# Five row buffers over the keys, the second set's scatters spread over the tiles, and the first set's results fetched two tiles sooner

## The chip, the cores and the metric

The kernel runs on one core of a Trainium2 chip. The core has five engines with an instruction queue each: TensorE (PE) multiplies, VectorE (DVE) and ScalarE (ACT) do elementwise work, GpSimd (POOL) does small elementwise work and issues the DMAs whose row addresses are data (indirect DMAs), and SyncE (SP) issues the plain DMAs. Each queue is worked off in its order; engines wait for each other by semaphores. The metric is the device time of one execution in microseconds: a median of 1357.8 over three runs of the kernel before, 1356.98 to 1358.16.

## The reference

One transformer block on 2 x 1024 rows of 256 numbers, all float32: an attention with 16 query heads and one key/value head, and a mixture of 8 experts of which each row uses 2. Both stand behind a layer norm with a shift and a scale computed from a condition `c`, and both are added to `x` through a gate.

```python
mod = (silu(c) @ wmod).reshape(2, 6, 1, -1)        # sa, ca, ga, sb, cb, gb
h = layernorm(x) * (1 + ca) + sa
x = x + ga * attention(h)      # q, k normalised; 16 heads; out @ Wout; layernorm
h = layernorm(x) * (1 + cb) + sb
# experts
logits = h @ router_w.T
topk_vals, topk_idx = top_k(logits, 2)
topk_w = softmax(topk_vals)
x_sorted = h[order // 2]                           # rows sorted by expert
y1 = ragged_dot(x_sorted, w1, counts);  gate, up = split(y1, 2)
y2 = ragged_dot(silu(gate) * up, w2, counts)
y = (y2[inv] * topk_w).sum over the two choices
x = x + gb * y
```

## The kernel before

**Attention.** The 2048 rows are 16 row tiles of 128, and four query blocks of four tiles. For each block, `attention` (L469) runs over 16 heads and 8 key tiles: a score matmul (L478), its exponential on ScalarE (L482), a product with the values (L493). The keys of all rows lie transposed in one buffer, `kT` (8 KB in each partition); it stands first in the pool `big`, ahead of `vs` and the queries `qT`. `project` (L541) multiplies a block's heads by `Wout` (L547); `Settle` then normalises the result, adds it to `xs` (`residual`, L587), takes the second layer norm (`norms`, `logits`), the router's logits, and the two chosen experts with their weights (`weights`, L630).

**Sorting.** Each row goes to two experts. Where it stands in the list sorted by expert is counted in `count` and `bases`, and `scatter` (L741) writes a row tile of `rows` (256 numbers, the weight, the row that the result belongs to, and the batch) to those places in DRAM with an indirect DMA from POOL. There are two sets, so that the experts can begin before the last block is through: set 0 holds row tiles 0 to 11 and gives 31 sorted tiles of 128 rows, set 1 holds row tiles 12 to 15 (the last block) and gives 15. Set 0 is scattered during the last block's attention. For set 1 all of `residual`, `norms`, `logits`, `weights`, `count`, `bases` and its scatters take place in the expert stage, between the tiles. Its scatters come in two lots of four, one lot for each of a row's two choices; `choose_second` (L759) on POOL overwrites the weight and the destination in `rows` between the lots, and so waits until the first lot has been read.

**The expert stage.** It works through 46 sorted tiles in a loop over `m` (L1015). In step `m`, tile `m` is loaded seven steps ahead (`PRE`) and transposed (`turn`: xp on PE, its copy xT on ACT); tile `m-1` is multiplied by its expert's `w1` (`up`: su on PE, sg on ACT, sact on DVE); tile `m-3` is transposed back (`turn_back`: ap on PE, sactT on ACT); tile `m-4` (`LAG`) is multiplied by `w2` (`down`: sy on PE), scaled by weight and gate on DVE into `ysb` (L963, `self.evicted`), and written to its rows of `results` in DRAM by an indirect DMA from POOL (L966). `ysb` has four buffers and the PSUM tile `sy` two.

**Buffers.** The expert stage's pools take over the memory of the attention's. Three row tiles have buffers of their own outside both (`EARLY`, pool `mx`), and are loaded before the attention is over. All others, and the fetched results, share the 18 buffers of the pool `mr` (`row_buffer`, L887), which lie over `qT` and over the `proj` tile that `project` fills and `residual` reads.

**The results.** `fetch` (L987) reads the two results of each row of a row tile from DRAM (256 KB, SP queue), which is possible once all scatters of its set have landed; `combine` (L1001) adds both and `xs` on DVE, and writes the output (SP queue). For set 0 the loop fetches from m = 38 on, four row tiles in three steps (L1046), and combines each two steps later, behind the DVE instruction `evicted` of tile `m-4` (`tc.issue_after`). Set 1's four are fetched and combined after the loop.

The order within an engine's queue is made by a scheduler from the program's order, from dependencies and from these `issue_after` hints.

Of the kernel before, what the change touches and what calls it, by code (L numbers as in the profile page):

```python
# [38 lines left out]
FP = mybir.dt.float32  # L39
# [6 lines left out]
P = 128  # L46
# [9 lines left out]
def tile_adaln_attention_moe(  # L56
# [24 lines left out]
    QT = QB // P  # L81
# [8 lines left out]
    TOP = 2  # L90
    SETS = ((0, (NBLK - 1) * QT), ((NBLK - 1) * QT, NT))

    def tiles_for(n):

        return (TOP * n * P + E * (P - 1)) // P

    NM = [tiles_for(t1 - t0) for t0, t1 in SETS]
# [13 lines left out]
    WEIGHT, TO, BATCH, ROW = D, D + 1, D + 2, D + 4  # L111
# [5 lines left out]
    place_i = keep.tile([P, NT, TOP], I32, name="place_i")  # L117
# [82 lines left out]
    class Scattered:  # L200
# [3 lines left out]
        def __init__(self, name):  # L204
            self.name, self.all = name, []
# [19 lines left out]
    EARLY = 3  # L225
    mx = ctx.enter_context(tc.tile_pool(name="mx", bufs=1))

    with ExitStack() as attn:
# [440 lines left out]
        def count(blk, filled, work, psum, tag):  # L669

            t0 = blk * QT
            n = QT * TOP
            pairs = chosen[:, t0 : t0 + QT].rearrange("p t k e -> p (t k) e")
            ps = psum.tile([P, 2, n, E], FP, tag=tag, name=f"count_{blk}")
            for i, m in enumerate((before, ones)):
                nc.tensor.matmul(
                    ps[:, i].rearrange("p n e -> p (n e)"),
                    m,
                    pairs.rearrange("p n e -> p (n e)"),
                    start=True,  # L680
                    stop=True,
                )
            own = work.tile([P, n, E], FP, tag="z", name=f"own_{blk}")
            for i in range(n):
                nc.vector.tensor_tensor(own[:, i], ps[:, 0, i], filled, ALU.add)
                nc.vector.tensor_tensor(filled, filled, ps[:, 1, i], ALU.add)
            nc.vector.tensor_tensor(own, own, pairs, ALU.mult)
            nc.vector.tensor_reduce(
                place[:, t0 : t0 + QT].rearrange("p t k -> p (t k)"), own, AX.X, ALU.add
            )  # L690
# [50 lines left out]
        def scatter(to, i, t):  # L741
            ins = nc.gpsimd.indirect_dma_start(
                out=sorted_x[i],
                out_offset=bass.IndirectOffsetOnAxis(ap=to, axis=0),
                in_=rows[:, t, :],
                in_offset=None,
            )
            into_x[i].add(ins)
# [10 lines left out]
        def choose_second(t0, t1):  # L759

            nc.gpsimd.tensor_copy(rows[:, t0:t1, WEIGHT], share[:, t0:t1])
            nc.gpsimd.tensor_copy(rows[:, t0:t1, TO].bitcast(I32), second_to[:, t0:t1])
# [102 lines left out]
        w1_sb, w2s = w1_at  # L865

    with ExitStack() as moe:
        mg = moe.enter_context(tc.tile_pool(name="mg", bufs=3))
        ms = moe.enter_context(tc.tile_pool(name="ms", bufs=2))
        RING = 18  # L870
# [15 lines left out]
        PRE = 7  # L886
        def row_buffer(name):  # L887


            return mr.tile([P, TOP * D], FP, tag="x", name=name)  # L890

        class Sorted:


            def __init__(self, i, m):
                self.i, self.at = i, m
                self.m = m + sum(NM[:i])
                if self.m < EARLY:
                    self.x = mx.tile([P, ROW], FP, name=f"x_{self.m}")
                else:  # L900
                    self.x = row_buffer(f"x_{self.m}")[:, :ROW]
                load = nc.sync.dma_start(out=self.x, in_=sorted_x[i][ts(m, P), :])
                into_x[i].read(load)
# [40 lines left out]
            def down(self):  # L944
                m = self.m
                at = nc.values_load(
                    at_w2[self.i][0:1, self.at : self.at + 1],
                    engines=[mybir.EngineType.PE],
                    min_val=0,
                    max_val=(E - 1) * 2 * D,  # L950
                    skip_runtime_bounds_check_because="the expert's number is clamped",
                )
                y = ps_y.tile([P, D], FP, tag="y", name=f"sy_{m}")
                for c in range(2):
                    nc.tensor.matmul(  # L955
                        y,
                        self.actT[:, c, :],
                        w2_flat[:, c * D :][:, bass.ds(at, D)],
                        start=(c == 0),
                        stop=(c == 1),  # L960
                    )
                ysb = mg.tile([P, D], FP, tag="ysb", name=f"ysb_{m}", bufs=4)
                self.evicted = nc.vector.scalar_tensor_tensor(  # L963
                    ysb, y, self.x[:, WEIGHT : WEIGHT + 1], self.gate, ALU.mult, ALU.mult
                )
                ins = nc.gpsimd.indirect_dma_start(  # L966
                    out=results[self.i],
                    out_offset=bass.IndirectOffsetOnAxis(
                        ap=self.x[:, TO : TO + 1].bitcast(I32), axis=0
                    ),  # L970
                    in_=ysb,
                    in_offset=None,
                )
                into_results[self.i].add(ins)

            def gates(self):
# [10 lines left out]
        def fetch(t):  # L987

            i = 0 if t < SETS[0][1] else 1
            at = t - SETS[i][0]  # L990
            y = row_buffer(f"y_{t}").rearrange("p (k d) -> p k d", k=TOP)
            load = nc.sync.dma_start(
                out=y,
                in_=results[i][TOP * at * P : TOP * (at + 1) * P, :].rearrange(
                    "(p k) d -> p k d", k=TOP
                ),
            )
            into_results[i].read(load)
            return y

        def combine(t, y):  # L1001

            res = my.tile([P, D], FP, tag="res", name=f"res_{t}")
            nc.vector.tensor_tensor(res, y[:, 0, :], y[:, 1, :], ALU.add)
            nc.vector.tensor_tensor(res, res, xs[:, t, :], ALU.add)
            nc.sync.dma_start(out=ot[:, t, :], in_=res)
# [4 lines left out]
        which = [(i, m) for i, n in enumerate(NM) for m in range(n)]  # L1011
        tiles = []
        fetched, have = [], 0
        LAG = 4
        for m in range(len(which) + LAG):  # L1015
            while len(tiles) < min(m + 1 + PRE, len(which)):
                tiles.append(Sorted(*which[len(tiles)]))
            if m < len(tiles):
                tiles[m].turn()
            if 0 <= m - 1 < len(tiles):  # L1020
                tiles[m - 1].up()
            if 0 <= m - 3 < len(tiles):
                tiles[m - 3].gates()
                tiles[m - 3].turn_back()
            if 0 <= m - LAG < len(tiles):
                tiles[m - LAG].down()

            if m < QT:
                settle.residual(m, m + 1)
            elif m == QT:  # L1030
                settle.norms()
            elif QT < m <= 2 * QT:
                settle.logits(m - QT - 1)
            elif m == 2 * QT + 1:
                settle.weights()
            elif m == 2 * QT + 2:
                count(NBLK - 1, filled[1], mg, ps_t, "t")
            elif m == 2 * QT + 3:
                bases(1, mg)
                for k in range(TOP):  # L1040
                    if k:
                        choose_second(*SETS[1])
                    for t in range(*SETS[1]):
                        scatter(place_i[:, t, k : k + 1], 1, t)

            n = (m - (len(which) - 1 - PRE) + 1) * 4 // 3  # L1046
            for t in range(have, min(n, SETS[0][1])):
                fetched.append((m, t, fetch(t)))
                have = t + 1
            while fetched and fetched[0][0] <= m - 2:  # L1050
                with tc.issue_after(tiles[m - LAG].evicted.ins):
                    combine(*fetched.pop(0)[1:])
# [50 lines left out]
```

## Time and profile before

| what | value |
|---|---|
| median of three runs | 1357.8 us (1356.98 to 1358.16) |
| the profiled execution | 1363.5 us |
| its span, first to last instruction | 1361.8 us |
| PE busy | 1326.3 us, 97% |
| DVE / ACT / POOL busy | 685.6 / 489.0 / 229.4 us |
| PE's share of the chain that ended last | 93% |
| granted PE clock, mean | 0.989 |
| result scatters (L966, POOL) | 46, 1021 ns each |
| row loads (L902, SP) | 46 of 130 KB |
| result fetches (L992, SP) | 16 of 256 KB |

The span has four parts that can be told apart in the timeline: a start to about 60 us in which PE waits at times for loads and norms, the four attention blocks, the last block's out-projection until 1215.5 us, and the expert stage until the end. "The chain that ended last" is followed back from the last instruction, at each step to what released it. In the row of 40 slices each digit is the busy share of a slice of 34 us in tenths:

```
PE   7899999999999999999999999999999999989895
POOL 4200212110100000000100000001001233003543
```

### The profile page before, as it was taken

Reading aid. Unit: us, or ns where it says so; the run is one execution under the profiler, and the core shown is the slowest. Engines: PE = TensorE matmul, PEld = TensorE weight load, DVE = VectorE, ACT = ScalarE, POOL = GpSimd, SP = SyncE. Lnnn points to the kernel's source line nnn. Section 1 sums busy time; section 2 is a strip of 40 time slices with the busy share of each in tenths; the row PEclk is TensorE's granted clock in tenths of the full one; section 3 lists DMA queues with packets and bytes.
Section 4 is the critical chain, followed back from the end, with each engine's and each line's share of the span. In section 5 each row is a group of like instructions: output and inputs, shape, how many; then the busy total and the mean of one; then the engine's idle time right before and its main releaser. Section 6 shows DMA issues by size and latency. Waiting matters only on the chain.

```text
span 1361.8 us, 12740 instructions
## 1 busy us (share of the span) xinstructions
PE 1326.3 (97%) x4024; PEld 688.8 (51%) x4024; DVE 685.6 (50%) x1380; ACT 489.0 (36%) x954; POOL 229.4 (17%) x325
## 2 busy tenths in 40 slices
PE   7899999999999999999999999999999999989895
PEld 4444444446544444447444444466444444467674
DVE  6346655544545554533646454545465545347445
ACT  2433344442243333331343333422433333314342
POOL 4200212110100000000100000001001233003543
PEclk9899999999999999999999999999999999999998
DMA  7001000000004310101000210000000122013335
GB/s 243 1 0 31 1 32 0 20 12 32 1 1 156 57 32 0 31 1 32 0 1 31 85 32 1 31 32 0 1 32 0 55 65 91 1 43 118 122 124 191
DMA packets 46322, 59.18 MB, mean 43 GB/s; under 512 B 10672, under 2 KB 32432, under 8 KB 46256
## 3 DMA queue, kind: packets, MB, share of 16 engines
q1 hardware_dynamic: 42512, 48.08, 11.6%
q0 software_dynamic: 3744, 10.29, 2.1%
q8 instruction: 33, 0.54, 0.2%
q14 instruction: 33, 0.27, 0.1%
HBM read 39.69 MB, written 18.66 MB: 43 GB/s over the span
## 4 chain that ended last, share of the span: by engine, by line
PE 93%; DVE 2%; POOL 1%; DMA 1%; issue 1%; ACT 0%; another core or an unknown queue 0%; SPq 0%; POOLq 0%; DVEq 0%; ACTq 0%
PE s L478 32%; PE o L493 32%; PE q L441 8%; PE pr L547 7%; PE su L924 4%; PE sy L955 3%; PE qp L455 2%; PE den L507 1%; PE kv L384 1%; PE xp L909 1%; PE ap L940 1%; PE lg L625 0%; POOL rn_q L178 0%; PE warm_a L768 0%
## 5 line engine op out<-in xcount | busy, mean ns | idle before, releaser
L478 PE MATMUL s<-qT,kT 128*128 128x512 f32 x1024 | 525.3, 595 | 0.1
L493 PE MATMUL o<-p,vs 128*128 128x512 f32 x1024 | 522.7, 593 | 0.0
L482 ACT ACTIVATE p<-s 128x512 f32<-128x512 f32 x512 | 305.6, 597 | 502.4 <-PE s L478 487.1
L498 DVE TENSOR_TENSOR sum<-sum,p 128x512 f32<-128x512 f32 x384 | 264.3, 688 | 180.1 <-ACT p L482 175.6
L493 PEld LDWEIGHTS o<-p,vs 128*128 128x128 f32 x1024 | 193.4, 190 | 233.2 <-issue 232.0
L478 PEld LDWEIGHTS s<-qT,kT 128*128 128x128 f32 x1024 | 187.3, 191 | 206.2 <-issue 204.2
L177 POOL TENSOR_SCALAR rn_q<-rn_q 128x4 f32<-128x4 f32 x64 | 14.0, 219 | 719.9 <-DVE rn_q L344 704.8
L441 PE MATMUL q<-wq_sb,rows 128*128 128x512 f32 x256 | 121.0, 596 | 0.0
L547 PE MATMUL pr<-wout_sb,qT 128*128 128x256 f32 x512 | 112.7, 380 | 0.0
L547 PEld LDWEIGHTS pr<-wout_sb,qT 128*128 128x128 f32 x512 | 96.6, 190 | 18.9 <-issue 4.3
L498 DVE TENSOR_TENSOR sum<-p,p 128x512 f32<-128x512 f32 x64 | 44.2, 690 | 112.7 <-ACT p L482 112.6
L344 DVE TENSOR_REDUCE rn_q<-sq_q 128x4 f32<-128x512 f32 x64 | 43.8, 684 | 83.6 <-ACT sq_q L343 83.6
L178 POOL TENSOR_TENSOR rn_q<-rn_q,minus_half 128x4 f32<-128x4 f32 x64 | 83.3, 1302 | 5.3
L441 PEld LDWEIGHTS q<-wq_sb,rows 128*128 128x128 f32 x256 | 49.0, 192 | 60.4 <-issue 50.4
L347 DVE TENSOR_TENSOR vn_q<-q,rn_q 128x512 f32<-128x512 f32 x64 | 44.2, 690 | 58.2 <-POOL rn_q L178 58.2
L343 ACT ACTIVATE sq_q<-q 128x512 f32<-128x512 f32 x64 | 38.2, 597 | 75.2 <-PE q L441 70.8
L523 DVE TENSOR_TENSOR qT<-qT,wide 128x512 f32<-128x512 f32 x64 | 42.3, 689 | 45.3 <-DMA wide<-spread 45.2
L924 PE MATMUL su<-w_sb,xT 128*128 x184 | 64.1, 470 | 1.0 <-issue 0.9
L515 DVE RECIPROCAL rden<-den 128x512 f32<-128x512 f32 x16 | 53.7, 3357 | 20.0 <-PE den L507 20.0
L966 POOL DMA_INDIRECT results<-ysb,x x46 | 47.0, 1021 | 64.4 <-DVE ysb L963 47.4
L955 PE MATMUL sy<-w2s,sactT 128*128 x184 | 48.4, 387 | 3.5 <-ACT sactT L942 3.0
L455 PEld LDWEIGHTS qp<-ident,vn_q 128*128 128x128 f32 x256 | 32.3, 143 | 37.3 <-issue 31.2
(160 smaller groups left out, 767.9 us busy)
## 6 DMA issues: line engine op xcount, KB each, us to landing
wide<-spread SPq DMA_DIRECT2D x64, 256.0 KB
x<-sorted_x SPq DMA_DIRECT2D x46, 130.0 KB
y<-results SPq DMA_DIRECT2D x16, 256.0 KB
sorted_x<-zero SPq DMA_DIRECT2D x1, 4030.0 KB
w_sb<-in_w_dram SPq DMA_DIRECT2D x2, 1408.0 KB
wout_sb<-in_wout_dram SPq DMA_DIRECT2D x1, 2048.0 KB
out_dram<-res SPq DMA_DIRECT2D x16, 128.0 KB
sorted_x<-zero SPq DMA_DIRECT2D x1, 1950.0 KB
```

Of the source, the lines that this page charges most:

```text
L178: latest["pool"] = nc.gpsimd.tensor_tensor(out, out, minus_half[:, : out.shape[1]], ALU.pow).ins
L441: nc.tensor.matmul(q.rearrange("p h d -> p (h d)"), hT[:, self.blk * QT + i, c, :], wq_sb[:, c, ts(g, QB)], start=(c == 0), stop=(c == DC ...
L455: nc.tensor.transpose(tp[:, j, :], qn[:, j, :], ident)
L478: nc.tensor.matmul(s, kT[:, ts(b * NJ + j, P)], q.head(h), start=True, stop=True)
L482: nc.scalar.activation(p, s, AF.Exp)
L493: nc.tensor.matmul(outs[h], vs[:, b * NJ + j, :], p, start=(j == 0), stop=(j == NJ - 1))
L498: latest["vector"] = nc.vector.tensor_tensor(sums[h], first, p, ALU.add).ins
L515: nc.vector.reciprocal(rden, den)
L547: nc.tensor.matmul(ps, q.head(h)[:, ts(i, P)], wout_sb[:, h, :], start=(h == 0), stop=(h == HEADS - 1),)
L924: nc.tensor.matmul(u, self.xT[:, c, :], w1_flat[:, c * I2 :][:, bass.ds(at, I2)], start=(c == 0), stop=(c == DC - 1),)
L955: nc.tensor.matmul(y, self.actT[:, c, :], w2_flat[:, c * D :][:, bass.ds(at, D)], start=(c == 0), stop=(c == 1),)
L966: ins = nc.gpsimd.indirect_dma_start(out=results[self.i], out_offset=bass.IndirectOffsetOnAxis(ap=self.x[:, TO : TO + 1].bitcast(I32), axi ...
```

## The change

It has three parts, all in the expert stage.

1. A new pool `me`, opened first in the stage, holds five more row tiles in buffers of their own (`NEXT = 5`): tiles 3 to 7. Being first, it takes the first memory that the attention's pools leave, which is that of `kT`. The other pools of the stage begin 5.2 KB later. Tiles from 8 on use the 18 buffers of `mr`.
2. The eight scatters of set 1, issued together in step m = 11 before, are issued one in each of the steps 12 to 19, each behind that step's result scatter (`self.scattered`). `choose_second` comes ahead of the fifth.
3. Set 0's results are fetched from m = 36 on (the step index that `NM[0] + LAG` = 35 gives), three row tiles in two steps, where it was from m = 38, four in three. `combine` stays two steps behind its fetch.

```diff
     with ExitStack() as moe:
+
+        NEXT = 5
+        me = moe.enter_context(tc.tile_pool(name="me", bufs=1))
         mg = moe.enter_context(tc.tile_pool(name="mg", bufs=3))
...
-                if self.m < EARLY:
-                    self.x = mx.tile([P, ROW], FP, name=f"x_{self.m}")
+                if self.m < EARLY + NEXT:
+                    pool = mx if self.m < EARLY else me
+                    self.x = pool.tile([P, ROW], FP, name=f"x_{self.m}")
                 else:
                     self.x = row_buffer(f"x_{self.m}")[:, :ROW]
...
+                self.scattered = ins.ins
                 into_results[self.i].add(ins)
...
             elif m == 2 * QT + 3:
                 bases(1, mg)
-                for k in range(TOP):
-                    if k:
+
+            n = m - (2 * QT + 4)
+            if 0 <= n < TOP * QT:
+                with tc.issue_after(tiles[m - LAG].scattered):
+                    k, t = n // QT, SETS[1][0] + n % QT
+                    if k and t == SETS[1][0]:
                         choose_second(*SETS[1])
-                    for t in range(*SETS[1]):
-                        scatter(place_i[:, t, k : k + 1], 1, t)
-
-            n = (m - (len(which) - 1 - PRE) + 1) * 4 // 3
+                    scatter(place_i[:, t, k : k + 1], 1, t)
+
+            n = (m - (NM[0] + LAG)) * 3 // 2
             for t in range(have, min(n, SETS[0][1])):
                 fetched.append((m, t, fetch(t)))
                 have = t + 1
```

`QT` is 4 and `TOP` 2, so `2 * QT + 4` is 12.

## The prediction

> **What bounds the kernel now.** The page first: TensorE is busy for 97% of the span and carries 93% of the chain that ended last, so only stretches in which TensorE waits are worth anything. The row of forty slices shows them in the first 60 us, which the change does not touch, and behind 1215 us, in the expert stage, which it does. There I read the chain of waits in order of time:
>
> ```profile
> 1222.31 0.68 DVE xs L599 x2
> 1223.41 1.98 DMA x<-sorted_x
> 1225.39 0.64 PE xp L909 x2
> ...
> 1265.37 1.15 PE sy L955 x4
> 1268.63 4.29 issue
> 1273.62 1.10 PE sy L955 x4
> 1274.72 0.65 PE xp L909 x2
> 1275.49 4.19 another core or an unknown queue
> 1280.29 2.08 PE sy L955 x4
> ...
> 1349.85 2.39 DMA results<-ysb,x
> 1352.51 2.93 DMA y<-results
> ```
>
> (start, us, what.) The reader is to see two breaks and a tail. At 1220 the chain leaves TensorE for the residual's last addition and for a load of sorted rows. Around 1270 it leaves it again, for something not named. After the last tile stand a scatter, a fetch and the last stores. The table of stretches (sum over each, count in brackets, then the granted clock, DMA share, GB/s) shows the same breaks as lost TensorE time:
>
> ```profile
> core 0: us, PE busy (x) PEld busy (x) DVE busy (x) ACT busy (x) POOL busy (x), PEclk, DMA share, GB/s
> 1220.00:1240.00 20.00, 15.34 (x73) 10.87 (x71) 13.72 (x42) 6.14 (x18) 4.67 (x5) 0.91 0.48 140
> 1240.00:1260.00 20.00, 20.00 (x105) 15.14 (x106) 16.23 (x78) 10.27 (x27) 8.15 (x8) 1.00 0.28 83
> 1260.00:1280.00 20.00, 15.85 (x74) 11.18 (x72) 6.51 (x16) 5.23 (x17) 12.81 (x15) 1.00 0.43 137
> ```
>
> Undisturbed, a tile takes 2.49 us (the result scatters from 1296.19 to 1343.47 stand that far apart, TensorE without a gap).
>
> **Break one: the buffers over the keys.** The timeline of SP has one entry for the row loads, 18 of them from 1223.04 on, right behind the residual's last addition (1222.98): the first buffers of the ring lie over memory of the attention pools that this addition frees last. TensorE has done the three early tiles by 1220.72 and waits until 1225.38: 4.66 us, and the clock is granted at half for 3.41 us behind it. After the change tiles 3 to 7 lie over the keys; in the built program their first load waits for the last out-projection matmul (1215.50 in the trace), not for the addition. From issue to use a load took 2.35 us (1223.04 to 1225.39), so tile 3 is there at about 1217.9, before TensorE wants it. **What is late next** is VectorE: the first activation of a tile (sact_0) comes at 1221.73 to 1222.05 whatever the loads do, since it stands behind the residual. So ap_0 starts at 1222.05 and TensorE idles 1.25 us. I walk the rows on with the trace's own steps (xp 0.22, su 1.18, ap 0.22, sy 0.87 us from start to start; su to silu 1.39; ap to its copy 0.77): sy_0 at 1223.9, sy_1 at 1226.4, then tp2_12 at 1227.3. It needs `rows` of block 3, which needs the rsqrt on POOL; in the built order two sact now stand ahead of the last statistics on VectorE, so the row comes at 1228.25 instead of 1227.6, and TensorE waits 1.0 us. ysb_0 is done by 1228.7, in time for sy_2 at 1230.57. The trace has sy_2 at 1234.88, and from there both run at the same 3.24 us per tile. **Gain 4.3 us.** The check by another way: 4.66 idle plus half of 3.41 at half clock, less the 1.25 and 1.0 that stay, is 4.1. Ends: 3.5 (VectorE's new order costs 0.8 more) and 4.9 (tp2_12 waits for nothing). Tiles 8 on still wait for the addition, at 1223, and are wanted at 1234: hidden. The memory of the expert stage's other buffers moves up by 5.2 KB; none of their waits lands later than the out-projection.
>
> **Break two: the scatters of the second set.** Before, POOL issues eight key scatters nearly in one go, with the result of tile 9 between, and results 10 to 15 queue behind:
>
> ```profile
> 1269.23 0.96 POOL L742 DMA_INDIRECT sorted_x<-rows,place_i  x1 [0.30 <-issue]
> 1270.49 0.96 POOL L966 DMA_INDIRECT results<-ysb,x  x1 [0.30 <-issue]
> 1272.99 0.48 DVE L963 SCALAR_TENSOR_TENSOR ysb<-sy,x,gate 128x256 f32<-128x256 f32 x1 [4.36 <-DMA results<-ysb,x]
> 1275.45 0.37 ACT L911 COPY xT<-xp 128x256 f32<-128x256 f32 x1 [3.88 <-PE xp L909]
> 1279.66 0.32 ACT L932 ACTIVATE sg<-su 128x176 f32<-128x176 f32 x1 [3.84 <-remote]
> ```
>
> (two rows of POOL's timeline, one of VectorE's, two of ScalarE's; idle time and its releaser in brackets.) Result 10 leaves at 1270.49 and lands at 1272.9; ysb_14 wants its buffer, of four, so it comes at 1272.99; sy_16 wants the PSUM buffer that ysb_14 empties, so it starts at 1273.59 instead of 1272.44. That is **1.15 us**, and it follows from the program. The rest does not: sy_12 at 1262.48 to sy_18 at 1284.41 is 21.93 us for six tiles, 6.99 over 6 x 2.49. The 5.84 us beyond 1.15 come from ScalarE's two rows (and a smaller one at 1264.14): xp and su had been issued at 1271.31 and 1271.53, their inputs were there, and the copies that wait for them start about four and seven us late, with a clock at half behind it (1280.01, 3.41 us).
>
> After the change a key scatter stands behind each of results 8 to 15. POOL's cadence back to back is 1.265 us (1270.49, 1271.76, 1273.02), two per tile 2.53 against 2.49: it just keeps up. The two `choose_second` copies wait until the first four key scatters have landed, some 1.9 us with the gap behind. So POOL lags at most about 4.2 us behind VectorE (result 13 about 1270.5 for a ysb ready at 1266.3); a result then lands some 3 us ahead of the ysb that wants its buffer, four tiles or 10 us on. **The wait goes entirely**; the cover is those 3 us. The set's loads need the last key scatter, now at about 1277, and tile 31 is turned after 1300: hidden.
>
> **How much of the 6.99 the runs shown hold.** The profiled execution took 1363.5 us, 5.7 over the median of 1357.8. [...] the span from first to last instruction is alone 1361.8, 4.0 us over the median, so most of the excess is inside; and 5.84 us of unnamed lateness is nearly the excess. [...] the runs shown lack that lateness, and the term is 1.15. Ends: 0.3 and 7.0.
>
> **The tail and the fetches.** The first twelve results are fetched from m = 36 instead of 38, three per two tiles instead of four per three. In the built program the fetches from y_3 on still wait for the same tiles' scatters (y_3 for tile 31), so they move by little; two loads of x (130 KB each) now stand among y_0 to y_2, about 1 us on the queue. On VectorE the pairs of additions (0.42 us each, two pairs at most per tile of 2.49, beside 0.34 and 0.48) fit as they do now; y_3 would land at about 1329 for a use at 1330.7, and a late one has some 3.4 us before sy feels it. What leaves the tail are six of twelve additions that stand between ysb_42 and ysb_45: ysb_45 would be ready at 1348.7, not 1349.57. But POOL has its four last scatters at 1.265 us from 1345.73: the last at 1349.5 instead of 1349.85. With slightly freer DMA queues **0.45 us**, ends 0 and 1.2.
>
> **Sum.** Against the profiled execution: 4.3 + 7.0 + 0.45 = 11.7, that is 1351.8 (or 1357.6 if the unnamed lateness comes again). Against the median: 4.3 + 1.15 + 0.45 = 5.9, 1357.8 - 5.9 = **1351.9**.
>
> **Rivals.** (B) The unnamed lateness belongs to the kernel and goes with the burst: 1357.8 - 11.7 = 1346.1. For it: all of it lies in POOL's unbroken run of scatters[...]. Against: POOL's run afterwards is as long, and the excess of the profile would be unexplained. (C) The early loads are not early, or VectorE's order takes the gain back: 1.6 left, 1356.2. For it: VectorE is busy without a gap from 1218.4 to 1226. Against: the waits named above. (D) **Slower: POOL sets the pace.** Place: tiles 8 to 16, 16 scatters in eight tiles. If one costs c, POOL falls behind by 16c + 1.9 - 19.9 us; this is 2.2 at 1.265, and 3 more are covered, so ysb waits once it passes 5.2 (c = 1.45), and the kernel is slower once it passes 5.2 + 5.9 (c = 1.82). At c = 2.0 it is 14.0, a loss of 8.8 and 1360.7. For it: spacings of 1.4 to 1.6 at 1139 to 1142. Against: every back-to-back spacing of this stage is 1.26.
>
> **How the numbers follow.** A 0.60 (1350.6 to 1353.9 from the ends), B 0.25 (1344.9 to 1347.5), C 0.10, D 0.05. The range takes A and B: 1344.9 to 1354. A difference of 0.2%, 2.7 us, is about what a measurement of this kernel can tell from none. A and B are faster by more; C is within it; D slower: 0.86, 0.09, 0.05.
>
> **What would show it.** Row loads of tiles 3 to 7 near 1216 and no TensorE gap over 1.5 us there; sy_2 near 1230.6 if the attention ends at 1215.5 again; no ysb waiting for a results DMA near 1270; result and key scatters in turn at 1.26 us; last result scatter about 3.5 us behind ysb_42's. I am wrong if TensorE waits behind POOL, or if the profile and the median move by very different amounts from 11.7 and 5.9.

## The result and the profile after

The changed kernel takes **1352.79 us** (median of six, 1352.02 to 1353.75), the kernel before beside it 1357.76 (six, 1356.98 to 1358.16): a ratio of 0.9965, 95% interval 0.9955 to 0.9976, or 4.97 us. The forecast was 1351.9, a gain of 5.9. The profiled execution went from 1363.5 to 1353.75 us and its span from 1361.8 to 1352.0: 9.8 us where 11.7 were forecast. It is 4.2 us for tiles up to `sy_2`, less 0.8 lost again by `sy_12`, 7.0 behind it, 0.3 in the tail, less 0.4 of a later attention and 0.5 of a slower end, all of which the table of profiles below shows. Most of the 7.0 is not the change's doing, as the experiments show.

The same stretches of the expert stage as before, in the table by stretches (sum and count of each engine, granted clock, DMA share, GB/s), and under it one entry of SP's timeline:

```profile
core 0: us, PE busy (x) PEld busy (x) DVE busy (x) ACT busy (x) POOL busy (x), PEclk, DMA share, GB/s
1220.00:1240.00 20.00, 18.09 (x90) 12.30 (x88) 14.71 (x47) 7.58 (x23) 5.52 (x6) 1.00 0.49 147
1240.00:1260.00 20.00, 20.00 (x102) 15.26 (x102) 16.51 (x78) 10.49 (x28) 9.33 (x10) 1.00 0.20 63
1260.00:1280.00 20.00, 20.00 (x98) 14.99 (x97) 10.55 (x25) 8.23 (x25) 14.59 (x17) 1.00 0.45 141
```

```profile
1215.89 2.22 SPq L906 DMA_DIRECT2D x<-sorted_x  x5
```

In the first stretch PE is busy for 18.09 us where it was 15.34, and the clock, 0.91 before, is full. In the third it is busy throughout, 20.00 instead of 15.85 (how much of that is the change's is told below). The five early row loads are issued at 1215.89, right behind the last out-projection.

The chain of waits (start, us, what) around the first break and at the end:

```profile
1220.86 0.65 DVE proj L593 x2
1221.50 0.67 DVE proj L597 x2
1223.13 1.41 PE su L928 x4
...
1229.44 0.79 DVE rows L612 x2
1230.39 0.88 DVE rows L615 x2
1232.82 0.85 PE su L928 x2
```

```profile
1320.33 4.85 DMA out_dram<-res
...
1339.51 2.40 DMA results<-ysb,x
...
1343.03 4.22 DMA y<-results
```

Before, the chain left TensorE at 1222 for a load of rows and at 1268 for something unnamed. Now, up to 1320, it leaves TensorE only for VectorE: up to 1222, where the first activation stands behind the residual, and again near 1230, behind `rows`. From there to 1320 all its long pieces are TensorE's. Then it goes over the stores and additions of the first set's results (`out_dram<-res`, `res`), which the fetches have brought forward; before, it stayed with TensorE there. TensorE itself keeps its pace: from `sy_22` to `sy_45` it takes 52.58 us in both profiles. At the end stand the same scatter and fetch as before, with a longer fetch (4.22 instead of 2.93).

POOL's timeline of the changed kernel, where before eight scatters stood in two lots:

```profile
1262.15 0.96 POOL L742 DMA_INDIRECT sorted_x<-rows,place_i  x1 [0.30 <-issue]
1263.42 0.96 POOL L970 DMA_INDIRECT results<-ysb,x  x1 [0.30 <-issue]
1265.41 0.19 POOL L761 COPY rows<-share 128x4 f32<-128x4 f32 x1 [1.03 <-DMA sorted_x<-rows,place_i]
1265.54 0.18 POOL L762 COPY rows<-second_to 128x4 int32<-128x4 int32 x1
1266.13 1.23 POOL L742 DMA_INDIRECT sorted_x<-rows,place_i  x1 [0.41 <-DMA x<-sorted_x]
1267.67 0.96 POOL L970 DMA_INDIRECT results<-ysb,x  x1 [0.30 <-DVE sact L938]
1268.93 0.96 POOL L742 DMA_INDIRECT sorted_x<-rows,place_i  x1 [0.30 <-issue]
1270.19 0.96 POOL L970 DMA_INDIRECT results<-ysb,x  x1 [0.30 <-DVE sact L938]
```

Key and result scatters (L742, L970) take turns, 1.26 us apart. `choose_second` (L761, L762) opens one hole. Result 13 is ready at 1263.49 and leaves at 1267.67, so POOL lags by 4.2 us (from a result's readiness to its scatter). No `ysb` waits for it.

### The profile page after: what moved, and what is told of

Read it like the earlier page. It is cut to its first block, busy times and chain, and to the rows that moved or that the text cites. A ratio compares the mean times of both kernels' runs of the same rounds, so it can differ in the third digit from the quotient of the medians.

```text
span 1352.0 us, 12731 instructions
## 1 busy us (share of the span) xinstructions
PE 1322.1 (98%) x4024; PEld 686.6 (51%) x4024; DVE 685.4 (51%) x1380; ACT 489.4 (36%) x954; POOL 229.1 (17%) x325
## 3 DMA queue, kind: packets, MB, share of 16 engines
q1 hardware_dynamic: 42512, 48.08, 11.6%
## 4 chain that ended last, share of the span: by engine, by line
PE 93%; DVE 2%; DMA 2%; POOL 2%; issue 1%; ACT 0%; SPq 0%; POOLq 0%; DVEq 0%; ACTq 0%
PE s L478 32%; PE o L493 32%; PE pr L547 8%; PE q L441 8%; PE su L928 3%; PE sy L959 2%; PE qp L455 2%; PE den L507 1%; DMA out_dram<-res 1%; PE kv L384 1%; PE ap L944 1%; PE xp L913 1%; POOL rn_q L178 0%; PE lg L625 0%; DMA wmod_sb<-in_wmod_dram 0%
## 5 line engine op out<-in xcount | busy, mean ns | idle before, releaser
L970 POOL DMA_INDIRECT results<-ysb,x x46 | 46.4, 1009 | 54.2 <-DVE ysb L967 37.9
```

What stands on the lines that cost most here:

```text
L970: ins = nc.gpsimd.indirect_dma_start(out=results[self.i], out_offset=bass.IndirectOffsetOnAxis(ap=self.x[:, TO : TO + 1].bitcast(I32), axi ...
```

## The experiments

**First group: the parts alone.** Each takes the kernel before and one part of the change, or two. Four kernels and the kernel before ran on one chip.

`buffers_alone`:

```diff
-                if self.m < EARLY:
+                if self.m < EARLY + NEXT:
+                    pool = mx if self.m < EARLY else me
```

> The kernel before with the first part alone (five row buffers over the keys); scatters in two lots and fetches from m = 38 as before. Theory A (the terms add up, break one as the trace of the changed kernel has it): sy_2 stands 3.9 us earlier, 0.65 of it is lost again at tp2_13, and 3.4 us stay: median about 1354.4, gain 3.0 to 4.3. The burst of eight key scatters is still there, so ysb_14 still waits about 1.2 us for the buffer of result 10. Theory R (what is won early is lost at the burst, because TensorE only reaches the same late row sooner): gain under 1 us, 1357. If the unnamed 5.84 us of lateness at tiles 12 to 18 is a matter of the kernel, this profile shows it again (sy_12 to sy_18 about 22 us, against 14.9 without the burst and 16.1 with its 1.15 alone); if it was an accident of one execution, about 16.1.

`spread_alone`:

```diff
-                for k in range(TOP):
...
+            n = m - (2 * QT + 4)
+            if 0 <= n < TOP * QT:
+                with tc.issue_after(tiles[m - LAG].scattered):
```

> The kernel before with the second part alone (set 1's eight scatters one behind each of eight result scatters). Theory A (the timed runs hold only the 1.15 us that the buffer of ysb costs): 1356.6. Theory B (they hold the whole 6.99 us): 1350.8. Theory N (they hold none, other slack takes it up): 1357.8. In the profile sy_12 to sy_18 takes 14.9 us in all three; what differs is the timed median.

`fetch_alone`:

```diff
-            n = (m - (len(which) - 1 - PRE) + 1) * 4 // 3
+            n = (m - (NM[0] + LAG)) * 3 // 2
```

> The kernel before with the third part alone (first set's results fetched from m = 36, three in two steps). Theory A: the tail is 0.45 us shorter, 1357.3, last result scatter about 2.6 us behind the start of sy_45 where it was 2.9. Theory T (the last four fetches set the end and land no sooner, the profiled execution of the changed kernel gave 0.32 and took 0.54): 1357.8 to 1358.0. The burst is in this kernel: as for the first one, sy_12 to sy_18 about 22 us if the unnamed lateness belongs to the kernel, about 16.1 if not.

`buffers_and_spread` has the first two of these edits.

> The changed kernel without its third part (fetches from m = 38, four in three steps, as before). Theory A: 0.45 us slower than the changed kernel, 1353.2. Theory T (the third part gives nothing or costs): 1352.4 to 1352.8. The last result scatter should stand 2.9 us behind the start of sy_45 in both theories; what differs is when the last fetched rows land.

| kernel | median us (range) | ratio to before, 95% |
|---|---|---|
| before, 28 runs | 1364.93 (1362.75 to 1366.49) | |
| `buffers_alone` | 1360.84 (1359.80 to 1362.93) | 0.9972 (0.9962 to 0.9983) |
| `spread_alone` | 1362.67 (1360.22 to 1363.66) | 0.9983 (0.9975 to 0.9992) |
| `fetch_alone` | 1364.45 (1361.03 to 1365.59) | 0.9994 (0.9986 to 1.0003) |
| `buffers_and_spread` | 1359.15 (1357.81 to 1360.98) | 0.9957 (0.9943 to 0.9970) |

The surprise is the first row: on this chip the kernel before takes 7.2 us more than in the runs of the result. That level is also the level of the very first profile (1363.5). I call it the higher level, and that of the result the lower. So the ratios can be used, the absolute times of the expectations cannot. By the ratios the buffers are worth 3.8 us (2.3 to 5.2), the spreading 2.3 (1.1 to 3.4), both together 5.9 (4.1 to 7.8), so **the terms add up** as far as these intervals tell; theory R of the first run falls. The fetches, 0.8 with an interval that holds zero, stay undecided by time.

The profiles of all four lose time between tiles 12 and 22, `buffers_and_spread` too, which has no burst. So the unnamed lateness of the forecast was not confined to one execution, and spreading the scatters doesn't end it on this chip.

**Second group: is it the chip?** `before_again` and `changed_again` are the two kernels unchanged.

> The kernel before, unchanged, for a second profile. Theory C (the unnamed lateness belongs to the chip and the run of scatters together): on a chip on which the kernel before takes about 1365 us, sy_12 to sy_22 takes 31 to 33 us as in the first profile (31.88), and few of the semaphore events of that stretch are in the record; on one on which it takes about 1358 us, it takes 26.0 us (24.9 for ten tiles and 1.15). Theory E (an accident of single executions): no tie to the level of the chip.

> The changed kernel, unchanged, beside the same runs of the kernel before as its parts. Theory A (the terms add up on any chip): 5 us faster than the kernel before, ratio 0.9965. Theory C: on a chip at 1365 the profile shows late TensorE results from tile 12 on as in the kernel without the third part (sy_12 to sy_22 29.8 us) and the gain is 5 to 7 us; on a chip at 1358 it is 24.9 us and the gain 5 us.

`spread_thin`, over the changed kernel:

```diff
-            if 0 <= n < TOP * QT:
+            if 0 <= n < 3 * QT and n % 3 != 2:
+                n -= n // 3
```

> The changed kernel with the eight key scatters in eight of twelve steps (two steps of three) instead of eight in a row, so that POOL has 6.3 us of scatters in 7.5 us and pauses. Theory C (lateness needs POOL's unbroken run): on a chip at 1365 the profile loses under 2 us between sy_12 and sy_22 where the changed kernel loses 4 to 5, and it is 2 to 4 us faster than the changed kernel on the same chip; on a chip at 1358 it is equal to it. Theory D (POOL's pace matters in the timed runs of every chip): faster on both. Theory V (it is the volume of events, not the run): the loss is only stretched over more tiles, and the time is equal.

`settle_later`, over the changed kernel (the same for the other branches and for `n`):

```diff
-            if m < QT:
-                settle.residual(m, m + 1)
+            s = m - 1
+            if 0 <= s < QT:
+                settle.residual(s, s + 1)
```

> The changed kernel with the last block's chain (residual, norms, logits, weights, count, bases, key scatters) one step later in the loop. Theory S (the 0.65 us lost between sy_2 and sy_3 and the 0.29 us at tp2_12 are VectorE's order: ls of tile 12 stands behind ysb_1 and a gate): both go, and 0.5 to 1.0 us are gained over the changed kernel; the wait of ap_0 for sact_0 stays at 1.17 us, since sact_0 still stands behind the residual's products in the queue. Theory U (VectorE is simply full there): 0, only the place of the wait moves.

| kernel | median us (range) | ratio to before, 95% |
|---|---|---|
| before, 17 runs | 1365.24 (1362.77 to 1367.04) | |
| `before_again` | 1365.69 (1363.10 to 1366.57) | 1.0000 (0.9991 to 1.0009) |
| `changed_again` | 1357.62 (1357.30 to 1360.12) | 0.9947 (0.9933 to 0.9961) |
| `spread_thin` | 1356.58 (1354.95 to 1357.08) | 0.9931 (0.9917 to 0.9945) |
| `settle_later` | 1356.84 (1355.66 to 1357.87) | 0.9936 (0.9923 to 0.9950) |

This is another chip at the higher level, and again every profile has the lateness. Two rows of ScalarE's timeline in `changed_again`, idle time and its releaser in brackets:

```profile
1274.43 0.38 ACT L915 COPY xT<-xp 128x256 f32<-128x256 f32 x1 [2.31 <-PE ap L944]
1278.61 0.32 ACT L936 ACTIVATE sg<-su 128x176 f32<-128x176 f32 x1 [3.81 <-remote]
```

The same picture as in the first profile of the kernel before: ScalarE idles 2.31 and 3.81 us for products that start in TensorE's own rows at 1272.52 (`xp`) and 1272.74 (`su`), 1.91 and 5.87 us ahead of it. Where nothing is late, an activation starts 1.39 us behind its `su` (1269.04 and 1270.43 in the first profile). For the longer wait the releaser is only called "remote". The change is worth 7.2 us here (5.3 to 9.1) and 5.0 (3.3 to 6.1) in the runs of the result. A part of the lateness may go with the burst, but the intervals overlap, and most of it stays.

`spread_thin` takes 1.0 us less than `changed_again`, with ranges that just miss each other over five runs each, so pauses on POOL may help a little on such a chip; the 2 to 4 us of theory C did not come. `settle_later` takes 0.8 less, ranges overlapping.

**Third group.** By chance it ran on a chip at the lower level (the kernel before 1357.70, 12 runs, 1356.85 to 1358.88).

> The changed kernel once more, as the base for the three beside it. On a chip at which the kernel before takes 1365 us: 1357 to 1360, with 4 to 7 us of late TensorE results between sy_12 and sy_22; on one at 1358: 1352.8 and none.

`spread_thinner`, over the changed kernel:

```diff
+            upto = len(which) if m >= NM[0] - 3 else NM[0]
-            while len(tiles) < min(m + 1 + PRE, len(which)):
+            while len(tiles) < min(m + 1 + PRE, upto):
...
-            if 0 <= n < TOP * QT:
+            if 0 <= n < 2 * TOP * QT and n % 2 == 0:
+                n //= 2
```

> The changed kernel with one key scatter in every second step (16 steps instead of 8); for that the second set's row loads are issued from step 28 on instead of 24. POOL then has 3.8 us of scatters in 5.0. Theory C (the lateness grows with POOL's share in a run of scatters): on a chip at 1365 the loss between sy_12 and sy_22 falls further, 0 to 2.5 us where two steps of three gave 3.15 and the changed kernel 6.86, and the time is 1 to 4 us under the changed kernel's. Theory V (it is the number of semaphore events, whatever the run): the loss is stretched over twice the tiles, sy_12 to sy_30 loses as much as in the changed kernel, and the time is the same. On a chip at 1358 both give the changed kernel's time.

`settle_later_thinner` has this and the edit of `settle_later`.

> One key scatter in every second step, and the last block's chain one step later, over the changed kernel. If the two gains add (1.7 to 2 us for the later chain by sy_3 in its profile, 1 to 4 us for the thinner scatters where the lateness exists): 3 to 5 us under the changed kernel on a chip at 1365, about 1.5 on one at 1358. If the later chain's gain was noise: as the thinner scatters alone.

`spread_dense`, over the changed kernel:

```diff
-            if 0 <= n < TOP * QT:
+            for n in (2 * n, 2 * n + 1) if 0 <= n < QT else ():
```

> The changed kernel with two key scatters in each of four steps. Theory A (the reckoning of POOL's cover): POOL falls behind by 3 x 1.265 - 2.49 = 1.3 us a tile, 5.2 us over four, and 1.9 at choose_second, 7.1 in all, which passes the cover of 5.2; a ysb waits for its buffer, TensorE loses about 1.9 us, and the kernel is 1.5 to 3 us slower than the changed one on any chip. If POOL's lag has more cover than that: no difference on a chip at 1358. Theory C on a chip at 1365: POOL's run is unbroken for about the same length, so the late results stay at 5 to 7 us, and the wait comes on top in part.

| kernel | median us (range) | ratio to before, 95% |
|---|---|---|
| `changed_third` | 1352.74 (1352.35 to 1354.00) | 0.9965 (0.9953 to 0.9977) |
| `spread_thinner` | 1353.68 (1352.64 to 1354.40) | 0.9969 (0.9958 to 0.9980) |
| `settle_later_thinner` | 1352.32 (1352.15 to 1353.00) | 0.9960 (0.9947 to 0.9974) |
| `spread_dense` | 1352.83 (1351.40 to 1353.91) | 0.9963 (0.9949 to 0.9976) |

The result repeats itself: 4.96 us. No profile of this group has any lateness, and here the density of the scatters makes no difference that can be measured. What still thinner scatters do to the lateness, which this group was meant to ask, was therefore not measured. In `spread_dense` POOL falls even further behind than reckoned (result 12 is ready at 1261.17 and leaves at 1269.80, 8.6 us), and two rows of VectorE's timeline are late:

```profile
1268.52 0.48 DVE L967 SCALAR_TENSOR_TENSOR ysb<-sy,x,gate 128x256 f32<-128x256 f32 x1 [0.76 <-DMA results<-ysb,x]
1272.28 0.48 DVE L967 SCALAR_TENSOR_TENSOR ysb<-sy,x,gate 128x256 f32<-128x256 f32 x1 [2.04 <-PE ap L944]
```

But TensorE does not stop. `ysb_16` comes 1.64 us late and is done at 1272.76, and `sy_18`, which wants its PSUM tile, starts at 1274.55 as it would anyhow. Behind the four `ysb` buffers stands a second cover, the two PSUM tiles of `sy`, with 1.8 us of it left.

**The fourteen profiles side by side.** From the end of the attention (the last out-projection matmul): when `sy_2`, `sy_3` and `sy_12` start; what tiles 12 to 22 take beyond ten times 2.488 us; from the start of `sy_45` to the last result scatter; from there to the end of the span. All in us.

| profile | sy_2 | sy_3 | sy_12 | late, 12 to 22 | sy_45 to scatter | to the end |
|---|---|---|---|---|---|---|
| before | 19.38 | 22.62 | 46.98 | 7.00 | 2.91 | 11.95 |
| `before_again` | 19.32 | 22.56 | 46.91 | 8.76 | 2.91 | 12.17 |
| `fetch_alone` | 20.17 | 23.41 | 47.76 | 7.96 | 2.69 | 12.02 |
| `spread_alone` | 20.49 | 23.73 | 48.08 | 3.92 | 2.92 | 11.73 |
| `buffers_alone` | 15.19 | 19.07 | 43.75 | 6.17 | 2.92 | 12.40 |
| `buffers_and_spread` | 15.22 | 19.07 | 43.70 | 4.88 | 2.92 | 12.43 |
| `changed_again` | 15.18 | 19.07 | 43.74 | 6.86 | 2.59 | 11.65 |
| `spread_thin` | 15.18 | 19.06 | 43.59 | 3.15 | 2.74 | 12.44 |
| `settle_later` | 13.71 | 16.95 | 42.40 | 5.52 | 2.59 | 12.37 |
| after | 15.18 | 19.07 | 43.60 | 0.00 | 2.59 | 12.49 |
| `changed_third` | 15.18 | 19.06 | 43.58 | 0.01 | 2.59 | 11.92 |
| `spread_thinner` | 15.18 | 19.06 | 43.74 | 0.00 | 2.58 | 12.15 |
| `settle_later_thinner` | 13.70 | 16.95 | 42.33 | 0.00 | 2.58 | 12.14 |
| `spread_dense` | 15.18 | 19.05 | 43.57 | 0.01 | 2.58 | 12.23 |

Each column answers to one step of the forecast. The first three follow the buffers and, in two runs, the later chain of `settle_later`; among the four profiles with the old buffers they also follow the clock, granted at half for 3.41 us in `before` and `before_again` and for 6.83 in `fetch_alone` and `spread_alone`. The fifth follows the fetches, the last neither. From `sy_22` to `sy_45`, which no column has, it is 52.58 us in all but `fetch_alone` (53.08), `spread_thin` (53.19) and `settle_later_thinner` (53.34). The fourth is zero in the five profiles from the lower level and 3 to 9 us in the nine from the higher one, with or without the burst.

## Why the prediction was right, step by step

**Break one: right in mechanism, 0.9 too large against the first profile.** The loads leave at 1215.89 (forecast 1216), TensorE waits 1.17 us at `ap_0` (1.25) and `sy_2` stands 4.20 us earlier (4.3). The step that failed is "from there both run at the same 3.24 us per tile". From `sy_2` to `sy_3` the changed kernel takes 3.89. TensorE's timeline, and VectorE's beside it:

```profile
1228.40 0.41 PE L620 MATMUL tp<-ident,rows 128*128 128x128 f32 x2 [0.29 <-DVE rows L615]
...
1231.04 1.03 PE L959 MATMUL sy<-w2s,sactT 128*128 x4
1232.32 0.44 PE L620 MATMUL tp<-ident,rows 128*128 128x128 f32 x2 [0.25 <-DVE ls L628]
```

```profile
1231.18 0.48 DVE L967 SCALAR_TENSOR_TENSOR ysb<-sy,x,gate 128x256 f32<-128x256 f32 x1
1231.70 0.48 DVE L987 SCALAR_TENSOR_TENSOR gate<-gb_more,x,gb 128x256 f32<-128x256 f32 x1
1232.11 0.16 DVE L628 COPY ls<-lg 128x8 f32<-128x8 f32 x1
```

The transpose of `rows` for row tile 13 (L620; `tp2_12` is that of row tile 12) waits for a PSUM buffer that the copy `ls` of the row tile ahead frees, and this 0.16 us copy, whose products TensorE starts at 1229.61, comes at 1232.11, behind `ysb_1` and a gate on VectorE. In exchange the wait of `tp2_12` is 0.29, not 1.0. `settle_later` takes both away: in `settle_later_thinner` TensorE's rows have no wait at either transpose. As the chain stands one step later there, the transpose for row tile 12 now falls between `sy_2` and `sy_3` (3.25 us) and that for 13 between `sy_3` and `sy_4` (3.51), where the changed kernel takes 3.95 and 3.89:

```profile
1229.73 1.03 PE L959 MATMUL sy<-w2s,sactT 128*128 x4
1230.60 0.38 PE L620 MATMUL tp<-ident,rows 128*128 128x128 f32 x2
...
1232.98 1.03 PE L959 MATMUL sy<-w2s,sactT 128*128 x4
1233.84 0.38 PE L620 MATMUL tp<-ident,rows 128*128 128x128 f32 x2
```

So the order on VectorE is the cause. By `sy_12` the gain of the buffers is 3.38 us against the first profile. Against `spread_alone` it is 4.5, since there the clock is at half from 1223.08 to 1229.91, 6.83 us and not 3.41. Its row of the table by stretches, where the first profile has 15.34 us of PE and a clock of 0.91, reads

```profile
1220.00:1240.00 20.00, 15.71 (x70) 11.47 (x70) 12.70 (x39) 5.92 (x17) 4.67 (x5) 0.83 0.48 140
```

The forecast counted one stretch of 3.41 us. How long the clock stays down behind the wait for the loads differs between executions (3.41 or 6.83 us), and with it what the buffers are worth (3.38 or 4.5). `buffers_alone` measured 3.8 by its ratio. So 4.3 was inside what the part gives, and near its upper end.

**Break two: 1.15 fits the runs shown, the 7.0 of the profile came by luck.** No `ysb` waits, POOL's lag is 4.2 us as forecast, and the run from `sy_12` to `sy_22` is free of loss. The reading of the profile's excess held: the runs shown lack the other 5.84 us. What I did not see is that these belong to one of two levels at which the same kernel runs: `before_again` has them again, `changed_again` has them without the burst, and the five profiles from the lower level have none. By its time the first profile of the kernel before stood at the higher level, and the runs shown beside it at the lower. So the sum against the profile (11.7) counted as the change's what is the level's. That 9.8 us came all the same is luck: the profile of the changed kernel happened to be taken at the lower level. At the higher one its span was 1357.8. This is also the main reason why the profile gained 9.8 us and the median 4.97.

What remains for the spreading at the lower level is the rest of the sum: 4.97 less 3.38 for the buffers and 0.32 for the tail is 1.3, near 1.15. It is inferred, since no profile of the kernel before was taken at that level. The ratio's interval leaves some 1.5 us either way, and with 4.5 for the buffers, as against `spread_alone`, only 0.2 would remain. So the size of this term is not shown. Rival B needed 11.7 in the median, far outside the interval of 3.3 to 6.1, and rival C, with 1.6, lies below it.

That the first profile's excess over the median lay inside its span holds too: the profiled executions lie among the timed ones of their level (1353.75 with a median of 1352.79, 1352.55 with 1352.74), and time less span is 1.7 us in each of these profiles (1363.53 - 1361.8, 1353.75 - 1352.0, 1352.55 - 1350.8).

**The tail: 0.3 of the 0.45, and within the noise.** The last result scatter follows `sy_45` by 2.58 to 2.74 us with the new fetches and by 2.91 or 2.92 without. From there to the end it takes 11.65 to 12.49 us, with no tie to the part. So "slightly freer DMA queues" is not to be seen, and in the first profile after the gain of 0.32 was taken back by 0.54 of a slower end. The reckoning saw six of twelve additions leave the stretch from `ysb_42` to `ysb_45`; the trace before has eight there, the one after none.

The forecast left out what the earlier fetches bring forward: the stores of the output. `res` has four buffers, and VectorE now waits for one of them until its store has landed:

```profile
1325.21 0.43 DVE L1009 TENSOR_TENSOR res<-y 128x256 f32<-128x256 f32 x1 [1.66 <-DMA out_dram<-res]
```

All nine profiles with the new fetches have such waits in the loop, the longest 0.65 to 1.66 us in each, and none of the five with the old ones has any. In seven of the nine TensorE loses nothing by them before `sy_45`. In `fetch_alone` and `spread_thin` it loses 0.50 and 0.61 us at the last tiles, more than the tail gains; in `spread_thin` the row reads

```profile
1339.18 1.96 PE L959 MATMUL sy<-w2s,sactT 128*128 x8 [0.29 <-DVE ysb L967]
```

So the third part is not shown to be worth anything.

**Rival D** put the point from which POOL decides at 5.2 us of lag. `spread_dense` lags 8.6 and loses nothing. Two things were mis-sized. The 3 us that a result lands ahead of its `ysb` go with a lag of 4.2, not with the 2.2 to which I added them; with a lag of 8.6 `ysb_16` is only 1.64 late, so the `ysb` buffers cover 7.0. And the PSUM tile behind them, left out, covers 3.4 more. By these figures, as an estimate, POOL would decide from about 10.4 us of lag on. The kernel before agrees: its result 10, ready at 1259.64, left 10.9 us later, and `sy_16` waited.

**A version that beats both?** `settle_later_thinner` is 0.42 us under `changed_third`, with overlapping ranges, so it is not shown to be faster. In its profile 1.25 us are won by `sy_12` and 0.76 lost between `sy_26` and `sy_27`, where tiles 30 and 31 are turned and multiplied and the second set's loads leave only at 1291.51; that these are the cause was not tested. `settle_later` with the scatters as in the change keeps the 1.3 in its profile; it was 0.8 faster at the higher level, with overlapping ranges, and was not run at the lower one.

## What to carry to other kernels

Check first that the profile and the timed runs stand at the same level; if the profile's span alone exceeds the median, find the stretch that carries the excess and leave it out of the sum against the median. When a load is taken off the path, look for the wait that then ends last (here TensorE's 1.17 us for VectorE at `ap_0`), and at the small copies that free PSUM buffers: for `ls`, 0.16 us long, TensorE waited 0.25 us here. Look where such a copy stands in its engine's order. When a fetch is moved ahead, count the buffers of all that follows it, down to the last store (here VectorE waited up to 1.66 us for one of `res`). For the cover of a slower engine count every buffer between it and the bound one, here `ysb` with 7.0 us and then PSUM with 3.4, by the estimate above.

## What the runs showed of the hardware

Two levels, 1357.7 and about 1365 us for the same kernel, with an attention that ends at 1214.4 to 1216.1 us in both. Of the three chips of the experiments two stood at the higher and one at the lower, but each served one group of runs, so a level could also belong to the time and not to the chip. The changed kernel was profiled at both: its tiles 12 to 22 are 6.86 us late in `changed_again` and 0.01 in `changed_third`, and the spans differ by as much (1357.8 and 1350.8). In the first profile, at the higher level, semaphore events are recorded late and in bundles: six of TensorE stand within 0.25 us from 1279.64 on, where the changed kernel's first profile has them 0.22 to 1.19 us apart there, and the activation at 1279.66 starts with them, 8.13 us behind its products at 1271.53. The record also holds fewer of them. Over the whole span each of the five profiles from the lower level holds 8003 to 8014 semaphore events, each of the nine from the higher one 7093 to 7308. From 1260 to 1265 us the trace holds 119 in the changed kernel's first profile, 116 in `changed_third` and 31 in `changed_again`; from 0 to 60 us, where fewer are due, the counts agree within a few (548 to 555). A tie to POOL's scatters is not shown: with the changed kernel's pattern the lateness was 3.92, 4.88, 5.52 and 6.86 us in four profiles, thinned out 3.15 in one. What makes it, and whether it is there when nothing is recorded, stays open.
